# A graph layer on one core: VectorE fetches its columns one by one, and the turned table is made in the prologue

## The chip, the core and the metric

The kernel runs on one core of a Trainium2 chip. The core has five engines with instruction streams of their own: TensorE (PE; its weight loads are shown apart as PEld), VectorE (DVE), ScalarE (ACT), GpSimd (POOL) and SyncE (SP, which here only issues DMAs). [...] The metric is the device time of one execution, in microseconds, taken as the median of several runs.

## The reference

What is computed is one message-passing layer over a graph of 12500 nodes (48 features each) and 400000 edges (32 features each). The edges are sorted by their destination `dst`; the source `src` is arbitrary.

```python
h   = relu(layernorm(x))                                   # 12500 x 48
tmp = concatenate([h[dst], h[src], edge_attr_32], axis=1)  # 400000 x 128
msg = relu(tmp @ W1 + b1) @ W2 + b2                        # 400000 x 48
out = x + segment_sum(msg, dst)                            # 12500 x 48
```

All numbers are float32.

## The kernel before, in words

**Tables.** `W1` has three parts, for the destination, the source and the edge. So the kernel first makes two tables in DRAM, `tab_a = h @ W1[:48] + b1` and `tab_b = h @ W1[48:96]`, both of 12500 rows of 128 floats. This is the prologue, `node_tables` (L91 to L207). It takes x in six slices (8, 16, 20, 20, 20 and 14 groups of 128 nodes); the inner `turn` (L157 to L168) transposes the normalized rows on PE and leaves them, after a relu, as `ht` tiles; `table` (L171 to L190) multiplies them with the weights `wb` or `wa` on PE, copies the product out of PSUM on ACT (L189) and DVE (L187), and stores it to DRAM on SP's queue (L190). All of `tab_b` comes first, then `tab_a`. Once `tab_b` is stored, POOL can begin to gather rows from it.

**Chunks.** The main part, `windows` (L210 to L556), goes through the edges in 391 chunks of 1024 edges, that is 8 tiles of 128. As the edges are sorted, the destinations of a chunk lie in a window of W = 80 nodes. For chunk c:

- `prepare(c)` (L379): SP loads three things, each by a DMA: the 80 rows of `tab_a` of the window (`rhs`, L386), the edge features (`lhs`, L391) and the destinations (`row`, L393). POOL gathers `tab_b[src]` for 7 or 8 of the tiles, one indirect DMA per tile (L400), into one of six buffers `gb`. DVE makes a one-hot matrix of the destinations in `lhs` (L408) and a second one, `hot`, the other way round (L415).
- `before(c)` (L422): PE multiplies `lhs` with `rhs` into PSUM (`pre`, L428): the destination's part and the edge's part of tmp @ W1.
- `hidden(c)` (L442): DVE adds the gathered source part (L447), ACT applies the relu (L451, L452).
- `fold(c)` (L455): PE sums the hidden rows by destination with `hot` (L460, L463), and `add(c)` (L466) adds that on DVE to a segment accumulator of 1024 nodes (L475).
- Every 12 chunks a segment is closed: a memset (L491), a copy of the part that overlaps the next (L493), the product with `W2` (L501, L502), the sum with x (L503), and a store on SP's queue (L507).

**Three ways for the source part.** Gathering all 8 tiles of a chunk on POOL is not the only way to a source row. Some tiles are got otherwise, so that POOL has 7 gathers in most chunks:

- *By columns.* `bt` is `tab_b` turned round and held in SBUF, [128 hidden, 12544 nodes]. The source part of an edge is one column of it. In each chunk 114 columns are copied into a tile `gt` [128, 128], at addresses that lie in registers: 54 by DVE in three parts of 24, 18 and 12, and 60 by ACT in two parts of 28 and 32 (`PARTS`, L54). A full `gt` takes the place of a gathered tile: PE adds its transpose to `pre` (`turned`, L438). The numbers of nodes are first loaded into the engine's registers from the table `last` (`numbers`, `load`), in batches of at most 32.
- *By rows.* SP issues 12 single-row DMAs a chunk (`RPART`) from `tab_b` into a tile `gs` (`rows`, L302); DVE adds it (L449).
- The lists `BYCOLS` and `BYROWS` say which chunks have such a tile as their last.

ACT copies one column with one instruction (L368). DVE takes two with one TENSOR_SCALAR on integers (L361): its main operand is `first`, two constants (-1, 0) in PSUM beside `wnum`, and its two per-partition operands are the two columns. As (-1 and a) xor b = a xor b, and (0 and a) xor b = b, the pair of places holds a xor b and b. One XOR over all pairs of a run (`part_pairs`, L375) makes a out of the first. There are 27 such instructions and 3 or more XORs in a chunk.

**Where bt comes from.** The turned table is made inside the loop. In each of chunks 0 to 12 (`BUILD` = 13) SP loads up to 512 KB of `tab_b` (`turn_load`, L311), PE transposes it in up to eight pieces (`turn`, L320) and ACT copies them into `bt` (L321). So columns begin with chunk 14 (`COLS`), and rows with chunk 3 (`ROWS0`).

**The order.** It is written by hand (`manual_schedule`): each engine does its instructions in the order in which the loop over c issues them. The body of the loop (L510 to L556) is a pipeline: it prepares chunk c, has PE work on `before(c - 1)`, `fold(c - 2)` and `turned(c - 1)`, then `hidden(c - 1)` and `add(c - 2)`. On DVE one chunk's order is: L408, loads for part 1, pairs of part 0, L415, loads for part 2, pairs of part 1, XORs of part 0, pairs of part 2, XORs of part 1, L447, loads for part 0 of the next chunk, XORs of part 2, L475.

Of the kernel before, what the change touches and what calls it, by code (L numbers as in the profile page):

```python
# [8 lines left out]
F32 = mybir.dt.float32  # L9
I32 = mybir.dt.int32  # L10
AF = mybir.ActivationFunctionType
ALU = mybir.AluOpType
# [4 lines left out]
P = 128  # L17
N, D, DE, HID, E = 12500, 48, 32, 128, 400000
NR = 98
NPAD = P * NR  # L20
ROWS = 99 * P
NT = E // P
T = 8
CE = T * P
NCH = (NT + T - 1) // T
W = 80
# [22 lines left out]
BUILD = (NPAD + CE - 1) // CE  # L49
COLS = BUILD + 1  # L50
ROWS0 = 3
END = NT // T

PARTS = (  # L54
    (True, 0, 24, 1), (True, 24, 18, 25), (True, 42, 12, 43),
    (False, 54, 28, 56), (False, 82, 32, 84),
)
PART = sum(n for _, _, n, _ in PARTS)
BASE = 116
RPART = 12  # L60

BT0 = 16512
# [4 lines left out]
SEG, NEXT, SEG2 = 130, 131, 132  # L67
PLACE0 = 133
# [22 lines left out]
def node_tables(nc, tc, keep, x, ident, w1, b1, tab_a, tab_b, loads, most, check, rest):  # L91

    slices = [(0, 8), (8, 16), (24, 20), (44, 20), (64, 20), (84, 14)]
    ns = len(slices)
# [3 lines left out]
    with ExitStack() as es:  # L98
        node = es.enter_context(tc.tile_pool(name="node", bufs=3))
        ps_t = es.enter_context(tc.tile_pool(name="ps_t", bufs=3, space=PSUM))  # L100
        ps_n = es.enter_context(tc.tile_pool(name="ps_n", bufs=3, space=PSUM))
# [21 lines left out]
        hts = []  # L123
# [67 lines left out]

        for i in range(ns + 3):
            if i < ns:
                centre(i)
            if 0 <= i - 1 < ns:
                scale(i - 1)
            if 0 <= i - 2 < ns:
                turn(i - 2)
            if i == ns + 1:
                most()  # L200
            if i == ns + 2:
                check()
            if 0 <= i - 3 < ns:
                table(i - 3, wb, tb_v, i >= ns)
        for j in range(ns):
            table(j, wa, ta_v, True)
# [3 lines left out]
def windows(nc, tc, gp, bt, ident, idx, x_t, tab_a, tab_b, dst, edge_t, w1, w2s, b2s, out_t):  # L210
# [3 lines left out]
    with ExitStack() as es:  # L214
# [14 lines left out]
        wmask = ps_w.tile([P, W + 2], F32, name="wnum")  # L229
        wnum = wmask[:, :W]  # L230
        nc.vector.tensor_scalar_add(wnum, wrow, -HALF)

        first = wmask[:, W:].bitcast(I32)
        nc.vector.memset(first[:, :1], -1)
        nc.vector.memset(first[:, 1:], 0)
# [34 lines left out]
        gts = {}  # L270
# [36 lines left out]
        def turn_load(i):  # L307

            n = min(T, NR - i * T)
            t = wp.tile([P, T, HID], F32, name="hid")  # L310
            nc.sync.dma_start(  # L311
                t[:, :n, :],
                tab_b[i * CE : i * CE + n * P, :].rearrange("(t p) h -> p t h", p=P),
            )
            return n, t

        def turn(i, n, t):
            p_t = ps_p.tile([P, T, HID], F32, name="pre")
            for q in range(n):
                nc.tensor.transpose(p_t[:, q, :], t[:, q, :], ident)  # L320
            nc.scalar.copy(  # L321
                bt[:, i * CE : i * CE + n * P], p_t[:, :n, :].rearrange("h t p -> h (t p)")
            )

# [14 lines left out]
        def column(at):  # L339

            at = at.with_bounds(
                min_val=BT0, max_val=BT0 + 4 * (N - 1), guaranteed_mod_val=0, out_of_modulus=4
            ) - BT0
            return bt8[:, bass.ds(at, 4)]

        odd = {}

        def columns(c, part):


            dve, first_of, _, _ = PARTS[part]
            nodes = regs.pop((c, part), [])
            step = 2 if dve else 1
            runs = {}
            for k in range(0, len(nodes), step):
                j, e = divmod((c - COLS) * PART + first_of + k, P)
                of = BYCOLS[j]
                if of not in gts:
                    gts[of] = gtp.tile([HID, P], F32, name="gt")
                if dve:  # L360
                    nc.vector.tensor_scalar(  # L361
                        gts[of].bitcast(I32)[:, e : e + 2], first,
                        column(nodes[k]).bitcast(I32), column(nodes[k + 1]).bitcast(I32),
                        op0=ALU.bitwise_and, op1=ALU.bitwise_xor,
                    )
                    runs.setdefault(of, [e, e])[1] = e + 2
                else:
                    nc.scalar.copy(gts[of][:, e : e + 1], column(nodes[k]).bitcast(F32))  # L368
            odd[c, part] = [(gts[of], *run) for of, run in runs.items()]

        def part_pairs(c, part):

            for gt, e0, e1 in odd.pop((c, part), []):
                two = gt.bitcast(I32)[:, e0:e1].rearrange("h (k t) -> h k t", t=2)
                nc.vector.tensor_tensor(  # L375
                    two[:, :, 0], two[:, :, 0], two[:, :, 1], op=ALU.bitwise_xor
                )
# [131 lines left out]
        with tc.manual_schedule():  # L509
            for c in range(NCH + 2):  # L510
                if c < NCH:
                    prepare(c)
                    if c < BUILD:
                        part = turn_load(c)
                    rows(c, st[c].pop("rows"))
# [3 lines left out]
                part_pairs(c, 0)  # L519
                columns(c, 2)  # L520
                part_pairs(c, 1)
# [18 lines left out]
                part_pairs(c, 2)  # L540
# [10 lines left out]
                if c < BUILD:  # L551
                    turn(c, *part)
# [130 lines left out]
def tile_gnn_preln(  # L683
# [62 lines left out]
    with tc.tile_pool(name="keep", bufs=1) as keep, tc.tile_pool(  # L746
# [71 lines left out]
        node_tables(nc, tc, keep, x, ident, w1, b1, tab_a, tab_b, loads, most, check, rest)  # L818
# [79 lines left out]
```

## Time and profile before

Three runs took 4980.82 to 4988.03 us, with a median of 4982.04.

| Of the profiled execution | |
|---|---|
| its own time | 4980.82 us |
| its span | 4979.1 us |
| instructions | 86617 |
| PE busy | 3257.7 us (65%) |
| DVE busy | 3487.1 us (70%) |
| ACT busy | 2818.9 us (57%) |
| POOL busy | 2639.4 us (53%) |
| mean granted clock of TensorE | 0.598 |
| DMA | 361.39 MB, mean 73 GB/s |
| single-row DMAs (L302) | 4608 |

The span is what the profiler saw between the first and the last instruction; the time has 1.7 us more around it. A group's line in the profile gives: source line, engine, operation, output<-inputs with partitions x elements, count | busy time in us, mean length of one in ns | idle time of the engine just before these instructions, and what ended most of it. "issue" means that the engine waited for nothing that the profile can see. An instruction's length there can overlap that of the next; the distance between two starts is its pitch. Register loads are not counted as busy: they show as idle time before the instruction behind them.

### The profile page before, as it was taken

What the parts mean: (1) busy time and instruction counts of PE and PEld (TensorE: products, weight loads), DVE (VectorE), ACT (ScalarE), POOL (GpSimd) and SP (SyncE); (2) the same over time, 40 slices, a digit from 0 to 9 for tenths busy, and PEclk for the clock granted to TensorE, in tenths of its full rate; (3) what the DMA queues carried; (4) which work ended last, traced back from release to release, by engine and by line L of the source; (5) the groups of instructions that cost most, each with busy time, mean ns of one, the idle gap of its engine ahead of it and who ended that gap; (6) DMA issues with size and microseconds to landing.
All of it is one profiled execution on the core that took longest, in us unless ns stands there. A gap on an engine that the chain in (4) does not pass through costs nothing.

```text
span 4979.1 us, 86617 instructions
## 1 busy us (share of the span) xinstructions
PE 3257.7 (65%) x14562; PEld 2939.7 (59%) x14562; DVE 3487.1 (70%) x13620; ACT 2818.9 (57%) x23299; POOL 2639.4 (53%) x2783
## 2 busy tenths in 40 slices
PE   4666666666667766666666666776666666566676
PEld 3556656566656655556665555665556556556565
DVE  3257777777777777777777777777777777777775
ACT  2145555556555555555555555555555556556554
POOL 5555555555555555555555555555555555555552
PEclk7665566555565565565555655555665656665656
DMA  4522222222222222222222222222222222222221
GB/s 171 143 80 70 69 69 68 68 66 70 71 69 68 66 69 67 69 71 68 67 69 67 72 69 67 69 66 66 71 68 68 68 67 68 72 69 68 69 66 44
DMA packets 213723, 361.39 MB, mean 73 GB/s; under 512 B 69954, under 2 KB 119252, under 8 KB 211876
## 3 DMA queue, kind: packets, MB, share of 16 engines
q0 software_dynamic: 88192, 180.75, 14.2%
q1 hardware_dynamic: 124704, 174.91, 11.8%
q14 instruction: 447, 3.66, 0.2%
q8 instruction: 120, 1.97, 0.2%
q10 hardware_dynamic: 260, 0.10, 0.0%
HBM read 336.02 MB, written 22.07 MB: 72 GB/s over the span
## 4 chain that ended last, share of the span: by engine, by line
DVE 23%; issue 20%; POOL 7%; ACT 7%; DVEq 5%; PE 3%; DMA 1%; ACTq 1%; another core or an unknown queue 0%; SPq 0%; POOLq 0%
DVE gt L361 14%; POOL gb L400 7%; ACT gt L368 6%; DVEq L284 4%; DVE hid L447 3%; DVE hot L415 2%; PE p_g L460 1%; DMA gb<-tab_b,srci 1%; PE pre L428 1%; DVE gt L375 1%; ACTq L284 1%; DVE lhs L408 1%; ACT hid L452 1%; DVE seg L475 1%; DVE xseg L503 0%
## 5 line engine op out<-in xcount | busy, mean ns | idle before, releaser
L400 POOL DMA_INDIRECT gb<-tab_b,srci x2755 | 2617.7, 950 | 2263.4 <-DVE hid L447 1022.0
L368 ACT COPY gt<-bt 128x1 f32 x22500 | 2366.5, 187 | 1760.0 <-issue 1740.8
L361 DVE TENSOR_SCALAR gt<-wnum,bt 128x2 int32<-128x2 int32 x10126 | 1999.8, 271 | 1129.6 <-issue 1096.9
L460 PE MATMUL p_g<-hot,hid 128*128 128x80 f32 x6250 | 1388.3, 412 | 1532.1 <-ACT hid L452 1134.3
L460 PEld LDWEIGHTS p_g<-hot,hid 128*128 128x128 f32 x6250 | 1310.6, 318 | 1621.3 <-ACT hid L452 1203.3
L428 PEld LDWEIGHTS pre<-rhs,lhs 112*128 112x128 f32 x6250 | 1270.8, 310 | 99.4 <-issue 88.7
L428 PE MATMUL pre<-rhs,lhs 112*128 112x128 f32 x6250 | 1304.1, 396 | 10.8 <-issue 7.5
L408 DVE TENSOR_SCALAR_CACHE_REDUCE lhs<-row,bw 80x1024 f32<-80x1024 int16 x391 | 495.5, 1267 | 65.5 <-DMA row<-in_dst 59.8
L447 DVE TENSOR_TENSOR hid<-pre,gb 128x896 f32<-128x896 f32 (+2 forms) x391 | 425.8, 1089 | 33.8 <-issue 18.1
L452 ACT ACTIVATE hid<-hid 128x896 f32<-128x896 f32 (+1 forms) x391 | 373.2, 954 | 109.1 <-DVE hid L447 76.8
L415 DVE TENSOR_TENSOR hot<-wnum,rel 128x640 f32<-128x640 f32 x391 | 318.0, 813 | 0.0
L438 PE MATMUL pre<-ident,gt 128*128 128x128 f32 x668 | 239.2, 461 | 87.5 <-remote 71.2
L375 DVE TENSOR_TENSOR gt<-gt 128x12 int32<-128x12 int32 (+7 forms) x1266 | 192.6, 161 | 104.8 <-DVE hid L447 70.0
L463 PE MATMUL p_g<-ident,deg 80*128 80x80 f32 x782 | 240.8, 410 | 2.9 <-issue 2.9
L438 PEld LDWEIGHTS pre<-ident,gt 128*128 128x128 f32 x668 | 179.3, 328 | 94.3 <-remote 76.1
L463 PEld LDWEIGHTS p_g<-ident,deg 80*128 80x128 f32 x782 | 206.4, 322 | 3.6 <-issue 3.6
L451 ACT ACTIVATE hid<-pre 128x128 f32<-128x128 f32 x334 | 90.3, 270 | 123.2 <-DVE hid L447 64.8
L475 DVE TENSOR_TENSOR seg<-seg,p_g 128x160 f32 x391 | 122.6, 314 | 41.5 <-remote 26.3
L501 PE MATMUL p_f<-seg,w2s 128*48 128x512 f32 (+1 forms) x134 | 121.3, 1006 | 0.4 <-DVE seg L475 0.4
L502 PE MATMUL p_f<-seg,b2s 1*48 1x512 f32 (+1 forms) x134 | 110.7, 921 | 0.0
L502 PEld LDWEIGHTS p_f<-seg,b2s 1*48 1x48 f32 x134 | 14.1, 154 | 101.5 <-issue 101.5
L503 DVE TENSOR_TENSOR xseg<-xseg,p_f 48x512 f32<-48x512 f32 (+1 forms) x67 | 44.9, 671 | 24.1 <-PE p_f L502 23.1
(69 smaller groups left out, 380.7 us busy)
## 6 DMA issues: line engine op xcount, KB each, us to landing
gs<-tab_b SPq DMA_DIRECT2D x4608, 0.5 KB
row<-in_dst SPq DMA_DIRECT2D x390, 160.0 KB
lhs<-in_edge_t SPq DMA_DIRECT2D x390, 128.0 KB
gb<-tab_b,srci POOLq DMA_INDIRECT x2755
rhs<-tab_a SPq DMA_DIRECT2D x391, 40.0 KB
xseg<-in_x_t SPq DMA_DIRECT2D x33, 192.0 KB
out_x<-xseg SPq DMA_DIRECT2D x33, 192.0 KB
hid<-tab_b SPq DMA_DIRECT2D x12, 512.0 KB
```

The lines of the kernel that those rows point to most:

```text
L284: got += nc.values_load_multi_w_load_instructions(last[c % P : c % P + 1, c // P, at + k : at + min(k + MOST, n)], engines=[engine], min_v ...
L361: nc.vector.tensor_scalar(gts[of].bitcast(I32)[:, e : e + 2], first, column(nodes[k]).bitcast(I32), column(nodes[k + 1]).bitcast(I32), op0 ...
L368: nc.scalar.copy(gts[of][:, e : e + 1], column(nodes[k]).bitcast(F32))
L400: nc.gpsimd.indirect_dma_start(out=gb[:, t, :], out_offset=None, in_=tab_b[:, :], in_offset=bass.IndirectOffsetOnAxis(ap=srci[:, c * T + t ...
L408: nc.vector.tensor_scalar(lhs[:W, : n * P], row[:, : n * P], bw[:, c : c + 1], None, op0=ALU.is_equal, op1=ALU.add, accum_out=deg[:, :1],)
L415: nc.vector.tensor_tensor(hot[:, :n, :], wnum.unsqueeze(1).to_broadcast([P, n, W]), rel[:, c * T : c * T + n].unsqueeze(2).to_broadcast([P ...
L428: nc.tensor.matmul(pre[:, t, :], s["lhs"][:K, t * P : (t + 1) * P], s["rhs"][:K, :], start=True, stop=c not in BYCOLS or t < n - 1,)
L438: nc.tensor.matmul(s["pre"][:, s["n"] - 1, :], gts.pop(c), ident, start=False, stop=True)
L447: nc.vector.tensor_add(h[:, :g, :], pre[:, :g, :], s["gb"][:, :g, :])
L452: nc.scalar.activation(h[:, :m, :], h[:, :m, :], AF.Relu)
L460: nc.tensor.matmul(p_g[:, 0, :], s["h"][:, t, :], s["hot"][:, t, :], start=t == 0, stop=t == n - 1)
L463: nc.tensor.matmul(p_g[:, 1, :], s["deg"], ident[:W, :W], start=True, stop=True)
```

## The change

- DVE's pairs and XORs go. Each of its 54 columns is copied by an instruction of its own, `nc.vector.tensor_copy`, as ACT's are; the addresses, the parts and the register loads stay where they were. The constants `first` go from PSUM, and `wnum` stays there alone.
- `turn_load` and `turn` go from the loop. In the prologue a new `turned(j)` stands between the `tab_b` and the `tab_a` tables: PE multiplies `wb` with the `ht` tiles the other way round, which gives the turned table directly, up to 512 nodes at a time (28 matmuls in all), and ACT and DVE in turn copy it from PSUM into `bt`, with a stride (node p x 98 + r is row r of partition p, so neighbours in PSUM lie 98 columns apart in `bt`).
- Columns begin with chunk 1 (14 before), rows with chunk 1 (3 before), and a chunk has 14 rows (12 before). So 346 tiles come by columns (334 before) and 42 by rows (36 before), and 2737 by POOL's gathers (2755 before).

```diff
-BUILD = (NPAD + CE - 1) // CE
-COLS = BUILD + 1
-ROWS0 = 3
+COLS = 1
+ROWS0 = 1
...
-RPART = 12
+RPART = 14
...
-SEG, NEXT, SEG2 = 130, 131, 132
-PLACE0 = 133
+SEG, NEXT, SEG2 = 132, 133, 134
+PLACE0 = 135
...
+        def turned(j):
+
+            r0, rb = slices[j]
+            bt_v = bt.rearrange("h (p r) -> h p r", r=NR)
+            for g in range(0, rb // 2, 4):
+                n = min(4, rb // 2 - g)
+                for k in range(2):
+                    p_n = ps_n.tile([P, 2, 2 * HID], F32, name="p_n")
+                    of = p_n.rearrange("h a b -> h (a b)")[:, : n * P]
+                    nc.tensor.matmul(
+                        of, wb[:, k, :],
+                        hts[j][: 2 * D, g : g + n, :].rearrange("k q p -> k (q p)"),
+                        start=True, stop=True,
+                    )
+                    r = r0 + 2 * g + k
+                    to = bt_v[:, :, r : r + 2 * n - 1 : 2].rearrange("h p q -> h q p")
+                    of = of.rearrange("h (q p) -> h q p", p=P)
+                    if k:
+                        nc.vector.tensor_copy(to, of)
+                    else:
+                        nc.scalar.copy(to, of)
...
         for j in range(ns):
+            turned(j)
+        for j in range(ns):
             table(j, wa, ta_v, True)
...
-        wmask = ps_w.tile([P, W + 2], F32, name="wnum")
-        wnum = wmask[:, :W]
+        wnum = ps_w.tile([P, W], F32, name="wnum")
         nc.vector.tensor_scalar_add(wnum, wrow, -HALF)
-
-        first = wmask[:, W:].bitcast(I32)
-        nc.vector.memset(first[:, :1], -1)
-        nc.vector.memset(first[:, 1:], 0)
...
-        def turn_load(i):
...
-            nc.sync.dma_start(
-                t[:, :n, :],
-                tab_b[i * CE : i * CE + n * P, :].rearrange("(t p) h -> p t h", p=P),
-            )
...
-        def turn(i, n, t):
-            p_t = ps_p.tile([P, T, HID], F32, name="pre")
-            for q in range(n):
-                nc.tensor.transpose(p_t[:, q, :], t[:, q, :], ident)
-            nc.scalar.copy(
-                bt[:, i * CE : i * CE + n * P], p_t[:, :n, :].rearrange("h t p -> h (t p)")
-            )
...
-                if dve:
-                    nc.vector.tensor_scalar(
-                        gts[of].bitcast(I32)[:, e : e + 2], first,
-                        column(nodes[k]).bitcast(I32), column(nodes[k + 1]).bitcast(I32),
-                        op0=ALU.bitwise_and, op1=ALU.bitwise_xor,
-                    )
-                    runs.setdefault(of, [e, e])[1] = e + 2
-                else:
-                    nc.scalar.copy(gts[of][:, e : e + 1], column(nodes[k]).bitcast(F32))
...
-        def part_pairs(c, part):
-
-            for gt, e0, e1 in odd.pop((c, part), []):
-                two = gt.bitcast(I32)[:, e0:e1].rearrange("h (k t) -> h k t", t=2)
-                nc.vector.tensor_tensor(
-                    two[:, :, 0], two[:, :, 0], two[:, :, 1], op=ALU.bitwise_xor
-                )
...
+            dve, first, _, _ = PARTS[part]
+            copy = nc.vector.tensor_copy if dve else nc.scalar.copy
+            for k, at in enumerate(regs.pop((c, part), [])):
+                j, e = divmod((c - COLS) * PART + first + k, P)
                 of = BYCOLS[j]
...
+                copy(gts[of][:, e : e + 1], bt8[:, bass.ds(at, 4)].bitcast(F32))
...
                     prepare(c)
-                    if c < BUILD:
-                        part = turn_load(c)
                     rows(c, st[c].pop("rows"))
...
                 columns(c, 1)
-                part_pairs(c, 0)
                 columns(c, 2)
-                part_pairs(c, 1)
...
                 load(c + 1, 0)
-                part_pairs(c, 2)
...
-                if c < BUILD:
-                    turn(c, *part)
```

## The prediction, made before the kernel was run

> **What bounds the kernel now.** I read four views in turn: the page's costliest groups, DVE's and ACT's instructions in order of time over one chunk of mid-run, the waits of each engine, and POOL's gathers beside DVE's copies. First the groups (columns: line, engine, operation, out<-in, count | busy us, mean ns | idle us before them, and who ended it):
>
> ```profile
> L400 POOL DMA_INDIRECT gb<-tab_b,srci x2755 | 2617.7, 950 | 2263.4 <-DVE hid L447 1022.0
> L368 ACT COPY gt<-bt 128x1 f32 x22500 | 2366.5, 187 | 1760.0 <-issue 1740.8
> L361 DVE TENSOR_SCALAR gt<-wnum,bt 128x2 int32<-128x2 int32 x10126 | 1999.8, 271 | 1129.6 <-issue 1096.9
> ...
> L452 ACT ACTIVATE hid<-hid 128x896 f32<-128x896 f32 (+1 forms) x391 | 373.2, 954 | 109.1 <-DVE hid L447 76.8
> ...
> L375 DVE TENSOR_TENSOR gt<-gt 128x12 int32<-128x12 int32 (+7 forms) x1266 | 192.6, 161 | 104.8 <-DVE hid L447 70.0
> ...
> L451 ACT ACTIVATE hid<-pre 128x128 f32<-128x128 f32 x334 | 90.3, 270 | 123.2 <-DVE hid L447 64.8
> ```
>
> POOL waits for DVE to free gather buffers. ACT's columns wait on nothing named ("issue"). ACT waits for DVE only at the two relu lines: 109.1 + 123.2 = 232.3 us in the whole run. One chunk on DVE, in order of time (start, length, instruction, idle before it):
>
> ```profile
> 2508.82 1.09 DVE L447 TENSOR_TENSOR hid<-pre,gb 128x896 f32<-128x896 f32 x1 [0.59 <-issue]
> 2509.83 0.16 DVE L375 TENSOR_TENSOR gt<-gt 128x6 int32<-128x6 int32 x1
> 2509.90 0.32 DVE L475 TENSOR_TENSOR seg<-seg,p_g 128x160 f32 x1
> 2510.13 1.27 DVE L408 TENSOR_SCALAR_CACHE_REDUCE lhs<-row,bw 80x1024 f32<-80x1024 int16 x1
> 2511.33 0.08 DVE L408 DVE_READ_ACCUMULATOR lhs<-row,bw 80x1 f32 x1
> 2513.79 2.34 DVE L361 TENSOR_SCALAR gt<-wnum,bt 128x2 int32<-128x2 int32 x12 [2.38 <-issue]
> 2516.05 0.82 DVE L415 TENSOR_TENSOR hot<-wnum,rel 128x640 f32<-128x640 f32 x1
> 2517.08 1.78 DVE L361 TENSOR_SCALAR gt<-wnum,bt 128x2 int32<-128x2 int32 x9 [0.21 <-issue]
> 2518.77 0.17 DVE L375 TENSOR_TENSOR gt<-gt 128x12 int32<-128x12 int32 x1
> 2518.85 1.21 DVE L361 TENSOR_SCALAR gt<-wnum,bt 128x2 int32<-128x2 int32 x6
> 2519.98 0.16 DVE L375 TENSOR_TENSOR gt<-gt 128x9 int32<-128x9 int32 x1
> ```
>
> DVE's only idle time is behind its own register loads: 2.38 us before the first pairs, 0.21 before the second. It waits for no other engine, so DVE sets the pace: 390 periods from the first L408 (132.5 us) to the last (4949.1) average 12.35 us. The pairs start 188 ns apart (12 of them from 2513.79 to 2516.05), the XORs cost 0.07 to 0.08 us.
>
> ACT is hardly behind. Its columns start 92.5 ns apart until a stretch begins where each costs 0.71 us:
>
> ```profile
> 2512.20 2.60 ACT L368 COPY gt<-bt 128x1 f32 x27
> 2515.09 0.19 ACT L368 COPY gt<-bt 128x1 f32 x1 [0.29 <-issue]
> 2515.81 0.19 ACT L368 COPY gt<-bt 128x1 f32 x1 [0.52 <-issue]
> ...
> 2520.06 2.51 ACT L368 COPY gt<-bt 128x1 f32 x26 [0.53 <-issue]
> ```
>
> Such stretches end about 1.45 us after the last gather of a POOL burst (here the last began at 2517.70), and none shows after the last gather of the run (4910.9 us). So they follow POOL's bursts, whatever the cause inside the chip.
>
> **The change, part by part.** *DVE's columns.* Out go 27 pairs and 3 XORs a chunk: 27 x 0.188 + 3 x 0.076 = 5.31 us, in 375 chunks (10126 / 27), 1991 us. In come 54 one-column copies. The trace has none on DVE. The nearest rows: one-element TENSOR_SCALARs in the prologue start 0.071 (L811 to L813) and 0.075 us apart (L801 to L802), small XORs 0.073 to 0.08; a copy with a register address, seg at L493, starts the next instruction after 0.095 us, but carries 160 elements, so that is the upper end. Lower end 0.044: twelve pairs and L415 left DVE's sequencer within 0.57 us of the load's end. I take 0.073. Columns now run in 388 chunks: 388 x 54 x 0.073 = 1530 us, so DVE gets 460 us back (ends: 1070 back and none). The loads keep their places and sizes, with their gaps.
>
> Next in line, if nothing else comes, is ACT. A DVE that is never late gives it at most its 232 us; the longest of these waits (11.5, 9.2 us) lie at the ends and around segment changes and stay in part. I count two thirds, -155 (ends 0 and -232; beyond only if ACT's own gaps shrink, rival two).
>
> *What the copies do to POOL.* Seventeen of 2755 gathers took over 1.0 us, and each had the copy at L493 in it, the only regular copy of DVE's from SBUF to SBUF. One of them, POOL's answer first, DVE's below:
>
> ```profile
> 1381.96 0.95 POOL L400 DMA_INDIRECT gb<-tab_b,srci  x1 [0.30 <-issue]
> 1383.21 1.39 POOL L400 DMA_INDIRECT gb<-tab_b,srci  x1 [0.30 <-issue]
> ```
>
> ```profile
> 1383.61 0.18 DVE L493 COPY seg<-seg 128x160 f32 x1
> ```
>
> The gather ends 0.98 us after the copy's start, at whatever point it was hit, as if it began again; the copy itself is not late. No pair ever does it: a pair's main operand lies in PSUM. The new copies go from SBUF to SBUF, as L493 does. Upper end of the price: every copy of one element does what L493's does. Then a gather ends only 0.98 us after the start of the last copy of a stream. A chunk has two streams, 24 copies (1.75 us) and 30 (2.19 us), with L415 and a load gap between them (2516.05 to 2517.08 above: 1.03 us). A gather and its gap take 1.25 us (0.95 + 0.30). If one gather fits between the streams, the first ends at 1.68 + 0.98 = 2.66 us, the next at 1.75 + 1.03 + 29 x 0.073 + 0.98 = 5.88, and the other five of a chunk's seven need 6.25: 12.13 us. If none fits, six follow after 5.88: 13.38 us. Without the stop a chunk's gathers take 7 x 1.25 = 8.75. Lower end: one element is too short to matter, 0. The nearest row is L493: same engine, same operation, same two memories, same kind of address, only longer. I take it, and of its two periods the mean, since the room, 1.03 + 0.07 against 0.98, is less than the load gap varies (0.2 to 0.3): 12.75 us, more than DVE's 12.35 before. POOL becomes the bound.
>
> The Trainium skill ("SBUF — State Buffer", Who interferes with whom) says that a DVE copy in a two-port mode and GpSimd exclude each other, the first holding the ports for its whole instruction. By that the copies would wait too, up to a gather for each of two streams, 1.9 us a chunk, and the sum would be about 4981 + 388 x (1.9 - 1.37) = 5187; L493 starts 0.76 us after the memset before it inside a gather or outside, so here the row decides.
>
> *Columns from chunk 1, 14 rows.* (389 x 114) // 128 = 346 tiles against 334 come by columns, (389 x 14) // 128 = 42 against 36 by rows: 18 gathers fewer. Each lengthens a burst by 1.25 us (0.95 + 0.30 idle), in which ACT does at 0.71 what else takes 0.0925: about 1.1 us each, -20 (ends -22, 0). Twelve more column tiles make the first 13 periods, now (282.1 - 132.5) / 13 = 11.5 us, as long as the rest, some 12: +6 (ends 0, +12). SP issues 42 x 128 = 5376 rows for 4608; its rows take 6.7 us per 12 from 300 us on, so 768 cost some 430 us of queue. Cover: SP now waits 271.8 + 140.5 us before rhs (L386) and 611.5 before the output stores (L507), and issues the row load 10 to 27 us before DVE reads it. 0 (end +50, were stores to catch up too late). DVE's adds at L449 grow by 6 x 0.28 = 2 us.
>
> *The turned table.* Out of the loop: 13 loads from tab_b on SP, 98 transposes on PE, 13 copies of 1.0 us on ACT, all in chunks where DVE idles for row loads: 0 (end -13). Into the prologue, ahead of tab_a on PE: 28 matmuls of up to 512 columns, each about 1.06 us (the pair of records at L501, 196.39 us), with 14 copies each on ACT (0.59) and DVE (0.69; L189, L187), their strided store not seen before. That is 28 x 1.06 = 30 us of PE. Now tab_a's 25 groups start at 44.5; 16 are out by 59.7, and the other nine take until 118, because gathers run from 50.5 to 110 and PE stalls in them as ACT does (13.0 us busy between 60 and 110). With the new work in front, about half of it is done by 60, the rest creeps to the end of the burst (44 gathers, 50.5 + 55 = 105.5), and tab_a's 25 groups follow at 0.86 us: 107 + 25 x 0.86 + a few = about 133. +15 (ends 0; +58 if all 30 us and a doubled store fall behind the burst).
>
> *Sum.* The profiled execution took 4980.8 (span 4979.1 and 1.7 around it; the median of three is 4982.0). With POOL as the bound the parts on DVE and ACT are covered, and the end is POOL's: it begins chunk 6 when the first hid frees a buffer (140 before, +15 = 155), has 385 chunks at 12.75 = 4909, and some 16 us follow the last gather's chunk: 155 + 4909 + 16 = 5080. That is 99 more than 4980.8.
>
> **Rivals.** *One, the other side: one-element copies leave POOL alone.* Then DVE's 460 us come back and ACT is next: 4980.8 - 155 - 20 + 6 + 15 = 4827. For it: L493 moves 160 elements, a new copy one; a port that is taken for so short a time may be missed by the gather. Against: the gather at L493 loses up to its whole length to a copy of 0.18 us, so it isn't the copy's length that it pays. It decides wherever POOL needs less than (4981 - 171) / 385 = 12.49 us a chunk; if the stop holds and one gather always fits between the streams, 155 + 385 x 12.13 + 16 = 4841 is faster too, up to a copy of 0.080 us (0.36 more in 53 copies).
>
> *Two: ACT's own gaps shrink too.* No stop, and ACT's relus and the 0.70 us behind them (261 us, a register load), which now follow DVE's add at the start of a burst, lag some 4 us into the 0.71 stretch, where they cost few columns: 4827 - 261 = 4566. Against: PE's folds would then be issued there as well, and at 149 to 163 us one fold crept for 14 us.
>
> *Three: no change in effect.* No stop, and 0.095 a copy: 388 x 54 x 0.095 = 1990, DVE gets nothing. 4980.8 - 20 + 6 + 15 = 4982 (4940 to 5040).
>
> **How the numbers follow.** Forecast 0.56: from 4841 (one gather always fits) to 5322 (155 + 385 x 13.38 + 16, none does); 0.08 of it faster, 0.03 level, 0.45 slower, of which 0.08 above 5340 (copies dearer than 0.073). Rival one 0.27, faster (4640 to 4900). Rival two 0.04, faster. Rival three 0.13: 0.02 faster, 0.05 level, 0.06 slower. Faster 0.41, same 0.08, slower 0.51, with 0.2% (10 us) taken as what a measurement of this kernel tells from none. The range leaves out rival two, a quarter of rival one and what lies above 5340: 4760 to 5340. The forecast's own range is 4841 to 5322.
>
> **What would show it.** POOL: gathers' mean well above 950 ns, long ones wherever DVE's copies lie, its waits on DVE hid gone; DVE idle before hid with POOL as the releaser. If gathers still take 950 ns and POOL still waits for DVE, the step that L493 stands for a one-element copy is wrong. DVE: about 20,950 copies some 0.073 us apart; L375's XORs gone. ACT: waits at the relu shorter under rival one, longer under the forecast. Prologue: first L408 near 147 us. Wrong most easily: the stop, of which only a 160-element copy tells.

## The result, and the profile after

The changed kernel takes 5235.27 us (median of four runs, 5232.24 to 5236.9) where the kernel before takes 4981.66: 1.0505 of it, with a 95% interval of 1.0487 to 1.0524. That is 254 us slower. The forecast was slower, 5080.

The costliest groups of the changed kernel (columns as before: line, engine, operation, out<-in, count | busy us, mean ns | idle us before them and who ended it; each kernel has line numbers of its own):

```profile
L374 POOL DMA_INDIRECT gb<-tab_b,srci x2737 | 2595.8, 948 | 2533.5 <-DVE hid L421 1583.0
L351 ACT COPY gt<-bt 128x1 f32 x23282 | 2441.0, 187 | 1944.6 <-issue 1924.5
...
L351 DVE COPY gt<-bt 128x1 f32 x21006 | 1417.7, 145 | 1815.8 <-issue 1794.0
...
L426 ACT ACTIVATE hid<-hid 128x896 f32<-128x896 f32 (+1 forms) x391 | 372.9, 954 | 67.9 <-DVE hid L421 40.2
L389 DVE TENSOR_TENSOR hot<-wnum,rel 128x640 f32<-128x640 f32 x391 | 321.6, 822 | 158.0 <-issue 153.8
...
L449 DVE TENSOR_TENSOR seg<-seg,p_g 128x160 f32 x391 | 125.8, 322 | 250.3 <-DVE hid L421 204.8
...
L425 ACT ACTIVATE hid<-pre 128x128 f32<-128x128 f32 x346 | 96.1, 278 | 203.1 <-DVE hid L421 192.9
```

The gathers still take 948 ns (950 before), and POOL waits for DVE more than before, 1583 us instead of 1022. So the copies don't hold the gathers up, and DVE still sets the pace. Two gathers of the chunk that follows, with 24 one-element copies beside them (from 2508.52 on), are as long as any:

```profile
2508.65 0.95 POOL L374 DMA_INDIRECT gb<-tab_b,srci  x1 [0.30 <-issue]
2509.90 0.95 POOL L374 DMA_INDIRECT gb<-tab_b,srci  x1 [0.31 <-issue]
```

What changed on DVE is seen best in order of time, one chunk:

```profile
2502.29 1.08 DVE L421 TENSOR_TENSOR hid<-pre,gb 128x896 f32<-128x896 f32 x1
2504.08 0.32 DVE L449 TENSOR_TENSOR seg<-seg,p_g 128x160 f32 x1 [0.71 <-DVE hid L421]
2504.32 1.27 DVE L382 TENSOR_SCALAR_CACHE_REDUCE lhs<-row,bw 80x1024 f32<-80x1024 int16 x1
2505.52 0.08 DVE L382 DVE_READ_ACCUMULATOR lhs<-row,bw 80x1 f32 x1
2508.52 1.65 DVE L351 COPY gt<-bt 128x1 f32 x24 [2.93 <-issue]
2510.73 0.82 DVE L389 TENSOR_TENSOR hot<-wnum,rel 128x640 f32<-128x640 f32 x1 [0.56 <-issue]
2512.33 0.28 DVE L351 COPY gt<-bt 128x1 f32 x3 [0.77 <-issue]
2513.59 1.73 DVE L351 COPY gt<-bt 128x1 f32 x27 [0.98 <-issue]
2515.23 1.08 DVE L421 TENSOR_TENSOR hid<-pre,gb 128x896 f32<-128x896 f32 x1
```

The copies are cheaper than forecast: they start 0.061 us apart. But there are five idle times in this chunk, where the chunk shown in the prediction has three (0.59, 2.38 and 0.21 us). ACT's columns in the same chunk:

```profile
2505.51 2.70 ACT L351 COPY gt<-bt 128x1 f32 x27 [0.99 <-issue]
...
2510.73 0.28 ACT L351 COPY gt<-bt 128x1 f32 x2 [1.14 <-issue]
2512.15 0.28 ACT L351 COPY gt<-bt 128x1 f32 x2 [1.13 <-issue]
2513.57 2.50 ACT L351 COPY gt<-bt 128x1 f32 x26 [1.14 <-issue]
```

This is the stretch that the prediction described: ACT gets one column per 0.71 us, or two per 1.42. DVE's one-hot `hot` starts at 2510.73, at the same moment as ACT's two columns, and DVE's last 27 copies start at 2513.59 when ACT's stretch ends at 2513.57. So DVE's new idle times lie in the same stretches.

I added up the gaps between DVE's instructions by what stands on both sides of them, over some 365 chunks from 400 us on, in us per chunk:

| | before | after | difference |
|---|---|---|---|
| busy | 9.02 | 7.23 | -1.79 |
| idle before the columns of part 0 (load of 18 registers) | 2.68 | 2.80 | +0.12 |
| idle before the columns of part 1 (load of 12) | 0.33 | 0.98 | +0.65 |
| idle behind hid (load of 25) | 0.28 | 0.64 | +0.36 |
| idle before hot | 0 | 0.41 | +0.41 |
| idle inside the columns | 0 | 0.89 | +0.89 |
| idle before hid | 0.05 | 0 | -0.05 |
| period, from one L408 (L382 now) to the next | 12.40 | 12.99 | +0.59 |

The small rest of each column lies at the changes of segment. Over the 377 periods after the 13th the two spans differ by 377 x 0.604 = 228 us. The first L408 (L382 now) is 14.6 us later (147.1 for 132.5), the first 13 periods are 11.1 us longer together (160.7 for 149.6), and 1.5 us are at the end: 255 us, the difference of the spans, 5233.9 - 4979.1.

The new idle time is of two sorts. One is register loads, +1.13 us. The other is new, +1.30 us before hot and inside the columns, and falls into the stretches.

### The profile page after: what moved, and what is told of

Read it like the earlier page. It is cut to its first block, busy times and chain, and to the rows that moved or that the text cites. A ratio compares the mean times of both kernels' runs of the same rounds, so it can differ in the third digit from the quotient of the medians.

```text
span 5233.9 us, 98859 instructions
## 1 busy us (share of the span) xinstructions
PE 3314.1 (63%) x14544; PEld 2975.5 (57%) x14544; DVE 2881.0 (55%) x23252; ACT 2920.8 (56%) x24094; POOL 2617.5 (50%) x2765
## 5 line engine op out<-in xcount | busy, mean ns | idle before, releaser
L351 ACT COPY gt<-bt 128x1 f32 x23282 | 2441.0, 187 | 1944.6 <-issue 1924.5
L434 PE MATMUL p_g<-hot,hid 128*128 128x80 f32 x6250 | 1409.7, 418 | 1763.2 <-ACT hid L426 1526.9
L351 DVE COPY gt<-bt 128x1 f32 x21006 | 1417.7, 145 | 1815.8 <-issue 1794.0
L434 PEld LDWEIGHTS p_g<-hot,hid 128*128 128x128 f32 x6250 | 1327.9, 323 | 1857.5 <-ACT hid L426 1610.7
L402 PEld LDWEIGHTS pre<-rhs,lhs 112*128 112x128 f32 x6250 | 1283.9, 313 | 109.1 <-issue 89.9
L382 DVE TENSOR_SCALAR_CACHE_REDUCE lhs<-row,bw 80x1024 f32<-80x1024 int16 x391 | 495.7, 1268 | 12.2 <-DMA row<-in_dst 7.6
L421 DVE TENSOR_TENSOR hid<-pre,gb 128x896 f32<-128x896 f32 (+1 forms) x391 | 422.3, 1080 | 0.2
L465 DVE MEMSET seg<- 128x944 f32 x64 | 54.1, 845 | 9.6 <-issue 0.6
```

Of the source, the lines that this page charges most:

```text
L351: copy(gts[of][:, e : e + 1], bt8[:, bass.ds(at, 4)].bitcast(F32))
L382: nc.vector.tensor_scalar(lhs[:W, : n * P], row[:, : n * P], bw[:, c : c + 1], None, op0=ALU.is_equal, op1=ALU.add, accum_out=deg[:, :1],)
L402: nc.tensor.matmul(pre[:, t, :], s["lhs"][:K, t * P : (t + 1) * P], s["rhs"][:K, :], start=True, stop=c not in BYCOLS or t < n - 1,)
L421: nc.vector.tensor_add(h[:, :g, :], pre[:, :g, :], s["gb"][:, :g, :])
L434: nc.tensor.matmul(p_g[:, 0, :], s["h"][:, t, :], s["hot"][:, t, :], start=t == 0, stop=t == n - 1)
```

## The experiments

Runs of one set shared a chip and its runs of the kernel before. This matters here: the kernel before took 4810 us in the first set and 4982 to 5013 in all others. Each of these sets ran on a chip of its own. A ratio below is always to the runs of before in its own set. The first set's four traces lack the stretches: ACT's idle time in its columns with "issue" is 438 to 542 us there, against 1741 in the first profile of before, and no two of its columns start 0.6 to 0.8 us apart. The kernel before left no trace in that set.

**First set: without the stretches.** Undo the copies alone in the changed kernel (`after_pairs`), or make the copies alone in the kernel before (`before_singles`).

```diff
-                copy(gts[of][:, e : e + 1], bt8[:, bass.ds(at, 4)].bitcast(F32))
+                    nc.vector.tensor_scalar(
+                        gts[of].bitcast(I32)[:, e : e + 2], first,
+                        column(nodes[k]).bitcast(I32), column(nodes[k + 1]).bitcast(I32),
+                        op0=ALU.bitwise_and, op1=ALU.bitwise_xor,
+                    )
```

> The changed kernel with DVE's pairs and XORs back; the prologue's turned table, columns and rows from chunk 1 and 14 rows stay. Theory A (the one-by-one copies alone make the loss, by what they expose on DVE): the loss goes, 4960 to 4985 us, DVE's idle before L449's add and before the hot one-hot under 0.1 us a chunk each, none inside the column streams. Rival B (the loss comes from the other parts: 768 more row DMAs, 18 fewer gathers, the prologue): it stays above 5150 us.

> The kernel before with one-element copies for DVE's columns and nothing else changed. Theory A: 5220 to 5260 us, with the same idle times on DVE as in the changed kernel (0.4 us a chunk before the hot one-hot, 0.8 inside the columns of parts 1 and 2, 1.0 before part 1, 0.6 before the segment's add). Rival B: 4970 to 5000 us.

Measured: `after_pairs` 4895.53 us, 1.0177 (1.0160 to 1.0194) of before; `before_singles` 4727.07 us, 0.9830 (0.9813 to 0.9846). Theories and rivals all miss: here the copies are the better part and the rest of the change the worse. The trace of `before_singles` shows why. ACT's and DVE's columns run through:

```profile
2502.30 3.07 ACT L346 COPY gt<-bt 128x1 f32 x32 [0.94 <-issue]
2506.09 2.69 ACT L346 COPY gt<-bt 128x1 f32 x28 [0.73 <-ACT gt L346]
```

```profile
2505.30 1.55 DVE L346 COPY gt<-bt 128x1 f32 x24 [2.85 <-issue]
2506.77 0.81 DVE L384 TENSOR_TENSOR hot<-wnum,rel 128x640 f32<-128x640 f32 x1
2509.11 1.91 DVE L346 COPY gt<-bt 128x1 f32 x30 [1.53 <-issue]
```

DVE's idle time before hot and inside the columns is gone (0.02 us a chunk), while that of the loads is there in full (2.74, 1.54 and 0.65 us a chunk; period 11.95). So the two sorts of idle time have two causes.

**The number of instructions, and the places of the register values.** `after_twos` copies two neighbouring columns with each of 27 instructions. `after_aligned` moves the register values of each part to another place of the table that they are loaded from.

```diff
-            for k, at in enumerate(regs.pop((c, part), [])):
+            for k, at in list(enumerate(nodes))[::step]:
...
-                copy(gts[of][:, e : e + 1], bt8[:, bass.ds(at, 4)].bitcast(F32))
+                copy(gts[of][:, e : e + step], bt8[:, bass.ds(at, 4 * step)].bitcast(F32))
```

```diff
-    (True, 0, 24, 1), (True, 24, 18, 25), (True, 42, 12, 43),
-    (False, 54, 28, 56), (False, 82, 32, 84),
+    (True, 0, 24, 1), (True, 24, 18, 28), (True, 42, 12, 48),
+    (False, 54, 28, 60), (False, 82, 32, 88),
...
-BASE = 116
+BASE = 120
...
-WIDTH = 136
+WIDTH = 144
```

> The changed kernel with 27 copies of two neighbouring columns each in place of 54 of one: the second of each two is another node's, so this part of the computation is wrong; bytes and the kind of instruction stay, DVE's instructions halve. Theory A1 (during a burst of gathers instructions reach the engines slowly, so DVE pays for their number): the idle time inside columns 1 and 2 and before hot falls from 1.3 us a chunk to under 0.3, as it was with the 27 pairs. Rival A2 (a copy between SBUF tiles is itself held up while POOL gathers): it falls only by half, to about 0.6. Under both DVE's busy time falls by some 1.6 us a chunk and the time below 4950 us, unless the two-element copies stop the gathers, whose mean would then rise above 1.0 us.

> The changed kernel with the numbers of each part at a multiple of four in the table of register values (parts at 1, 28, 48, 60, 88 instead of 1, 25, 43, 56, 84; the table is 144 wide instead of 136). In both kernels DVE's register loads take 1.89 us for 25 registers at place 0, but 4.17 us for 18 at place 25 and 2.80 for 12 at place 43; ACT's 32 at place 56 take 2.01. Theory C (an odd place makes each register cost 0.23 us instead of 0.06 to 0.08): 18 registers then take 1.2 to 1.5 us and 12 take 0.8 to 1.0, DVE loses 2.5 to 3.5 us of idle time a chunk, and ACT or POOL sets the pace: 4500 to 4850 us. Rival (the length has another cause, such as the one-hot before it): 4.17 and 2.80 stay and so do 5235 us.

Measured: `after_twos` 4344.39 us in one run. As there were no stretches in this set, it says nothing on them. `after_aligned` 3517.15 us, 0.7314 (0.7302 to 0.7326), some 1000 us below the range expected. Its loads of 18 and 12 registers took 1.6 and 0.9 us instead of 4.17 and 2.80; DVE's idle time fell from 5.76 us a chunk (in the changed kernel's own profile) to 1.75, and POOL gathers one after another with 0.3 us between them, so that it sets the pace:

```profile
L374 POOL DMA_INDIRECT gb<-tab_b,srci x2737 | 2593.8, 948 | 866.3 <-issue 803.2
```

**Second set: is it the place, and is the loss the change's own?** The changed kernel and the one before as they are (`after_again`, `before_again`); the changed one with places 26 and 44 for 25 and 43 and nothing moved in SBUF (`after_even`; SBUF is the on-chip memory that holds most tiles, PSUM the one that PE writes to); and with the wider table alone (`after_wide`).

> The changed kernel as it is, once more. In the runs of the four kernels above, the kernel before took 4810 us and not 4982, and ACT's columns lost some 540 us to 'issue' where they lost 1741 and 1925 in the first two profiles: the stretches in which ACT gets one column per 0.71 us were nearly gone there. Theory D (the loss of the change comes from those stretches, which are not there in every run of a kernel): where they are missing, the two parts measured above multiply to 0.983 x 1.018 = 1.00, 4790 to 4840 us, and DVE's idle time inside its columns is under 0.1 us a chunk. Rival (the loss belongs to the change whatever the place): 1.05 of before, about 5050.

> The kernel before as it is, for its profile beside the others of this call. Theory D: ACT's idle time in its columns follows the time: about 540 us of 'issue' if it takes 4810 us, about 1741 if 4982. Rival: ACT's idle time is the same in both.

> The changed kernel with DVE's parts 1 and 2 at places 26 and 44 of the table of register values instead of 25 and 43; the table keeps its 136 columns, so no tile of the program moves in SBUF. Theory C1 (a register load from an odd place takes one slow access per register, an even place is enough): loads of 18 take 1.2 to 1.5 us, time 3500 to 3600 as with places that are multiples of four. Rival C2 (a multiple of four places is needed): the loads of 18 and 12 stay at 4.17 and 2.80 us, the time stays near that of the changed kernel. Rival C3 (the wider table of the kernel with the places at multiples of four moved other tiles, and that made the gain): loads get short but the time stays above 4300.

> The changed kernel with the table of register values 144 columns wide instead of 136 and every place as it was. Theory C1 and C2: the same time as the changed kernel in this call, within 0.5%. Rival C3 (where tiles lie in SBUF makes the gain): 3500 to 3700 us.

Here the stretches were back: before 5013.35, `before_again` 5012.54 with 1790 us of "issue" at ACT's columns. Measured: `after_again` 5279.69, 1.0530 (1.0512 to 1.0548), the first result once more; `after_wide` 5287.59 in one run; `after_even` 5270.29, 1.0514 (1.0496 to 1.0531). The width does nothing. In `after_even` the load of 12 from place 44 took 0.85 us, that of 18 from place 26 still 4.17: an even place isn't enough, a multiple of four is what the short loads have in common (0, 28, 44, 48, 56, 60, 84, 88). The 1.95 us that the shorter load saves a chunk brought nothing: idle time before part 1 fell from 0.95 to 0.03 us, and inside parts 1 and 2 it rose from 0.92 to 1.81. In the stretches DVE gives back what it gains elsewhere.

**Third set: the parts where the stretches are.** `before_singles`, the changed kernel, `after_twos` and `after_aligned` again.

> The kernel before with one-element copies for DVE's columns and nothing else changed, again, since what it does hangs on whether the 0.71 us stretches of ACT are there. Theory D: with the stretches (ACT's 'issue' idle near 1800 us, before near 5000) it is 4.0 to 6.5% slower than before, and DVE loses 1.2 to 1.5 us a chunk before hot and inside columns 1 and 2; without them (ACT's 'issue' near 530 us, before near 4810) it is 1.5 to 2% faster, as it was, and DVE loses nothing there. Rival E (the other parts of the change make its loss where the stretches are): 0.98 to 1.00 of before in both.

> The changed kernel as it is. Theory D: 1.045 to 1.055 of before with the stretches, 0.99 to 1.01 without them (0.983 from the copies times 1.018 from the rest). Rival (the loss of 5% is the change's own, wherever it runs): 1.05 in both.

> The changed kernel with 27 copies of two neighbouring columns in place of 54 of one (every second column is another node's, so this part of the computation is wrong). With the stretches, theory A1 (DVE pays for the number of its instructions there): idle time before hot and inside columns 1 and 2 under 0.3 us a chunk, where the changed kernel has 1.3. Rival A2 (it pays for the kind, a copy between SBUF tiles): about 0.6. Without the stretches 4344 us again, which tells nothing on this.

> The changed kernel with the numbers at multiples of four places. It took 3517 us where the stretches were missing; POOL was busy back to back there. Theory F (POOL's gathers set its pace: 391 x 7 x 1.25 = 3421 us and the prologue): 3500 to 3560 us wherever the stretches do not matter. With the stretches, if they come from POOL's gathers as such, nearly every column of ACT and DVE would fall into one and the time would go above 4500; if they are as long per chunk as now (some 5 us, of which ACT loses 4), 3900 to 4500.

Before took 4983.07. Measured: `before_singles_2` 5213.91, 1.0466 (1.0449 to 1.0484); `after_again_2` 5230.52, 1.0499 (1.0478 to 1.0520). So the copies alone make nearly all of the loss. They lose 0.40 us a chunk before hot and 0.97 inside the columns, as the changed kernel does.

`after_twos_2` took 4687.98 us in one run. Its idle time inside the columns is 0.04 us a chunk, before hot none. This chunk shows 15 copies running through in the middle of a stretch (ACT's steps last from 2509.88 to 2514.16 there):

```profile
2509.06 1.13 DVE L353 COPY gt<-bt 128x2 f32 x12 [2.85 <-issue]
2509.91 0.82 DVE L391 TENSOR_TENSOR hot<-wnum,rel 128x640 f32<-128x640 f32 x1
2512.35 1.15 DVE L353 COPY gt<-bt 128x2 f32 x15 [1.63 <-issue]
2514.27 1.09 DVE L423 TENSOR_TENSOR hid<-pre,gb 128x896 f32<-128x896 f32 x1 [0.77 <-PE pre L404]
```

They are copies from SBUF to SBUF as well, and as close in their starts (0.070 us). So it's the number of instructions that DVE pays for, not their kind.

`after_aligned_2` took 5071.48, 1.0180 (1.0163 to 1.0197): what gained 27% without the stretches is slower than before with them (above 4500, as was expected if nearly every column falls into a stretch). Its idle time inside columns 1 and 2 is 3.99 us a chunk. ACT and DVE move in the same steps, within 0.01 us of one another:

```profile
2513.48 0.28 ACT L351 COPY gt<-bt 128x1 f32 x2 [1.05 <-issue]
2514.22 0.19 ACT L351 COPY gt<-bt 128x1 f32 x1 [0.45 <-issue]
2514.92 0.19 ACT L351 COPY gt<-bt 128x1 f32 x1 [0.51 <-issue]
2515.64 0.19 ACT L351 COPY gt<-bt 128x1 f32 x1 [0.53 <-issue]
2516.35 2.78 ACT L351 COPY gt<-bt 128x1 f32 x29 [0.52 <-issue]
```

```profile
2513.49 0.22 DVE L351 COPY gt<-bt 128x1 f32 x2 [0.69 <-issue]
2514.22 0.15 DVE L351 COPY gt<-bt 128x1 f32 x1 [0.52 <-issue]
2514.93 0.15 DVE L351 COPY gt<-bt 128x1 f32 x1 [0.55 <-issue]
2515.64 0.15 DVE L351 COPY gt<-bt 128x1 f32 x1 [0.56 <-issue]
2516.36 1.43 DVE L351 COPY gt<-bt 128x1 f32 x22 [0.56 <-issue]
```

**Fourth set: where the stretches come from.** `after_spaced` is the changed kernel with a small memset on POOL behind each gather:

```diff
+        idle = one.tile([1, 448], F32, name="idle")
...
+                nc.gpsimd.memset(idle, 0.0)
```

`before_aligned` is the kernel before with the places of `after_aligned`, and `after_pairs_2` repeats `after_pairs`.

> The changed kernel with a small memset on POOL behind each gather (1 x 448 floats, some 0.46 us by the prologue's memsets), so that gathers start about 1.75 us apart instead of 1.25 and the seven of a chunk are spread over its period. Theory G (the stretches come from gathers close behind one another): ACT's 0.71 us steps are gone or rare, its idle time between columns falls from 4.05 us a chunk to under 1.5, DVE's before hot and inside its columns from 1.3 to under 0.3, and the time is set by POOL, 7 x 1.75 = 12.25 us a chunk: 4850 to 4950 us. Rival H (every gather holds instructions up for a time, whatever lies between them): the stretches stay or grow, 5200 us or more. Where there are no stretches to begin with (before near 4810), it tells nothing on this.

> The kernel before, with its pairs, and the numbers of each part at a multiple of four places (1, 28, 48, 60, 88). The loads of 18 and 12 registers take 1.6 and 0.9 us instead of 4.17 and 2.80. Theory A1 (27 pairs, 0.188 us apart, do not outrun the instructions that reach DVE in a stretch): DVE's idle time before part 0 falls from 2.68 to under 0.5 us a chunk, none appears inside the columns, and DVE's period goes to 9.0 busy + 0.5 unless ACT with 4 us lost in the stretches (11 to 11.6 us a chunk) is the bound: 4350 to 4700 us with stretches, 3600 to 3750 without. Rival (the stretches grow by what the loads give up, as in the changed kernel, 5071 against 5235): above 4800 with stretches.

> The changed kernel with DVE's pairs and XORs back, where it had 1.018 of before without the stretches. Theory A: with the stretches 1.000 to 1.010 of before, since the copies alone had 1.047 and the whole change 1.050 there; DVE has no idle time before hot and inside its columns. Rival B (the rest of the change costs as much as without the stretches): 1.015 to 1.02.

Before took 4987.27. `after_spaced` took 4830.93, 0.9691 (0.9672 to 0.9711), 400 us less than the changed kernel has where there are stretches. Its gathers start 1.57 us apart:

```profile
2508.86 0.95 POOL L375 DMA_INDIRECT gb<-tab_b,srci  x1 [0.16 <-issue]
2509.81 0.46 POOL L381 MEMSET idle<- 1x448 f32 x1
2510.44 0.95 POOL L375 DMA_INDIRECT gb<-tab_b,srci  x1 [0.16 <-issue]
```

Idle time between ACT's columns fell from 4.05 us a chunk to 1.17 (0.75 is what the first set has); its columns start 0.6 to 0.8 us apart 28 times in the whole run, and 1464 times in the changed kernel's. DVE's idle time before hot fell to none and inside the columns to 0.03. The first one-hot (L382 in the changed kernel) also came 40 us earlier, 106.7 for 147.1: between 60 and 110 us PE is busy for 32.3 us instead of 20.5. So on the chips that have stretches it is the closeness of the gathers that makes them; the first set, with the same 1.25 us, shows that it doesn't do so everywhere. The gathers themselves took as long as ever (952 ns). Against what was expected POOL is not the bound: seven gathers at 1.57 us need 10.99 us of a period of 12.05, and DVE still waits 4.95 us a chunk for its register loads.

`before_aligned` took 4779.23, 0.9585 (0.9569 to 0.9601). Its pairs don't wait in the stretches at all; ACT, with 4.16 us a chunk lost between its columns, now sets the pace (period 11.92), as the expectation had it, though 79 us above the range given there. `after_pairs_2` took 5009.31, 1.0048 (1.0031 to 1.0065): the rest of the change costs about 0.5% there, as theory A had it.

**Fifth set: both cures together.** The places of `after_aligned` with the memset of 448 floats, and with one of 256.

> The changed kernel with places at multiples of four and a memset of 1 x 448 floats on POOL behind each gather. A gather then starts 1.57 us after the one before (0.95 + 0.46 + 0.16), seven take 10.99 us a chunk. Theory (short loads take away what DVE waited for, spread gathers take away the stretches, and POOL is the bound): 155 + 385 x 10.99 + 16 = 4402, between 4380 and 4480 us, faster than either alone (4831 and 5071 where there are stretches). Rival (with POOL busy without a pause the stretches come back, as gathers never leave a gap): above 4700.

> The same with 1 x 256 floats, some 0.27 us: a gather every 1.38 us, 9.66 us a chunk on POOL. If a pitch of 1.38 us still keeps the stretches short, 155 + 385 x 9.66 + 16 = 3890, 3870 to 4000 us. If they come back at that pitch, ACT loses more than 2 us a chunk between its columns and the time is 4200 us or more.

Before took 4985.69. Measured: 4435.35 us, 0.8894 (0.8880 to 0.8909), and 4867.09, 0.9760 (0.9743 to 0.9776). The first is faster than both kernels. With the two, and `after_aligned_2` (another chip, also with stretches), there are three pitches of the gathers with the rest of the kernel the same: at 1.25 us ACT idles 4.22 us a chunk between its columns, at 1.41 us 3.11, at 1.57 us 0.81. Most of the gain lies between 1.41 and 1.57. The memset as such doesn't take the stretches away, since the one of 256 floats leaves them.

## Why the prediction was right and wrong

- *The bound.* Right for the kernel before: DVE set the pace. Its idle time is less simple than "2.38 us before the first pairs, 0.21 before the second": there is 0.28 us a chunk behind hid as well (the 104.8 us of L375's line), and the chunk shown has 0.59 before hid, which is rare (0.05 on average). Of the 232 us at ACT's relu lines 18.6 are "issue", no wait for DVE. For the kernel after, POOL was to be the bound with 12.75 us a chunk; DVE is, with 12.99.
- *The copies' own price.* The mechanism was right, the size off: 0.061 us apart and not 0.073, so DVE's busy time falls by 1.79 us a chunk, not 1.37.
- *"The loads keep their places and sizes, with their gaps."* Places and sizes, yes (4.17 and 2.80 us for 18 and 12 registers in both); the gaps, no. This is one step that failed. Twelve pairs take 2.3 us of DVE, and the load of the next part runs beside them: by the trace's record of it, in the chunk that the prediction shows, it began at 2514.26 and took 2.72 us, and only three of the twelve had started by then. 24 copies take 1.5 us, and the rest of the load lies open: 0.98 for 0.33 us. Behind hid the small XOR, and with it the add, went out at once in the chunk shown; now the add waits for the load: 0.64 for 0.28. `before_singles` has the same without any stretch (1.54, 0.65). The dearer instructions had been cover for the loads. These gaps were put at no change without a reason; they grew by 1.13 us a chunk.
- *What the copies do to POOL.* The step that carried the sum failed: L493's row doesn't stand for a copy of one element. The stop, priced at about 4 us a chunk on POOL (12.75 for 7 x 1.25 = 8.75), isn't there at all. In the changed kernel 825 gathers have such copies inside them, 8.4 on average and up to 16, and take 0.946 us on average. The 30 gathers over 1.0 us all have the 160-element copy (L467 now) in them. The rule of the Trainium skill that the prediction weighed ("SBUF — State Buffer", Who interferes with whom) would have one side wait if these copies ran in a two-port mode; in `before_singles`, where there are no stretches, neither side waits (gathers 946 ns, DVE's idle time inside the columns 0.02 us a chunk). No run shows in which mode they ran.
- *The sum.* 5080 against 5235, 99 us more than before where 254 were measured. That it came out slower, as forecast, was luck: the cost that made it so isn't there, and another of 1.13 + 1.30 us a chunk is. Rival one's condition held, POOL was left alone, yet its 4827 missed too. Both put at nothing the loads' gaps, +1.13 us a chunk, and left out that DVE would fall into the stretches that the prediction had itself described for ACT and PE, +1.30; where these are missing, the copies alone gave 0.983 of before. With DVE bound at 12.99, ACT had nothing to gain.
- *Rivals two and three.* Rival two's ACT gaps did not shrink (0.98 us behind the relus against 0.69). Rival three named a copy as dear as half a pair; it wasn't.
- *Rows, columns, prologue.* The first L382 came at 147.1 as forecast. SP's slack shrank (62 us of waits before rhs instead of 412) but covered the 768 rows. Together the rest of the change was put at +1 us; with stretches it measured 0.3 to 0.5%, some 17 to 24 us (5230.5 against 5213.9, and 1.0048). Without stretches it cost 1.8%, 86 us. `before_singles` has the prologue and the first 13 chunks of the kernel before, and set beside `after_pairs` it places some 60 of these 86: the first one-hot comes at 108.0 us instead of 81.4, and the 13 periods from there take 150.0 us instead of 116.7, as columns now begin with chunk 1. With stretches the same chunks take 149 us in `before_singles_2` and 152 in `after_pairs_2`, so the first chunks of before have little to lose there. The +6 for these periods was sized in stretches too, and measured 11.1 in the changed kernel.

What stays open: by what way gathers close to one another slow the other engines down, and why the first set showed nothing of it. The fetch of instructions, in blocks of 8192 bytes, looks alike in all traces (median 391 to 455 ns a block, 400 to 431 in the first set). That each engine draws on a small stock of instructions and gets one per 0.71 us once it is used up would fit the counts, 27 copies run through and 54 don't, but no run tests it.

## What to carry to other kernels

Instructions that take long on an engine can hide the register loads that run beside them: here twelve pairs of 2.3 us left 0.33 us of a load open, and 24 copies of 1.5 us left 0.98. Before replacing slow instructions by more and faster ones, ask which loads and waits they covered. Where an engine's stream stops for no named reason and another engine's stops in the same steps, count instructions rather than busy time, and try to spread what starts these stretches: a memset of 0.46 us behind each gather took nearly 8% off the changed kernel. Where there are no stretches it may cost: `after_aligned` took 8.69 us a chunk in the first set, and seven gathers 1.57 us apart need 10.99 (this was not run there). And a gain that is measured on one chip has to be seen on another: the change with the places moved took 0.73 of the time before in the first set and 1.02 in the third. Chip and time of the run can't be told apart in this.

## What the runs showed of the hardware

- *Register loads and places.* On DVE a load of 18 registers from place 25 or 26 of a row of 4-byte numbers took 4.17 us, from place 28 1.6 us; 12 took 2.80 from place 43 and 0.85 to 0.9 from 44 or 48. That is 0.23 us a register or 0.07 to 0.09. The Trainium skill ("Runtime: NRT & Kernel Launch", Instruction fetch mechanics) puts a TENSOR_LOAD, as the trace calls these loads too, at about 200 ns a register; it speaks of loads from HBM, and these read a table in SBUF. The runs come near it for the places that are no multiple of four, and are under half of it for the others.
- *Gathers and the other engines.* In the runs of the result and in four of the five sets POOL's gathers, 1.25 us apart, slowed the instructions of ACT and DVE to steps of 0.71 us, and PE in the prologue (20.5 us busy between 60 and 110 us, against 32.3); 1.57 us apart they hardly did. In the first set they didn't at 1.25 us either.
- *Copies and gathers.* In the changed kernel 30 of the 31 gathers with a DVE copy of 160 elements from SBUF to SBUF in them ended about 0.99 us after that copy's start, and lasted up to 1.53 us (1.91 in the kernel before); the 825 gathers with copies of one element in them took 946 ns.
